# Three bias rows as one-row products on TensorE, and a new order of a code transpose and of the steps before a top-51 choice

## The chip, the cores and the metric

The kernel runs on one core of one Trainium2 chip. The metric is the device time of one execution in microseconds (us), the median of the runs shown. The engines are named as in the profile: PE is TensorE (PEld its weight loads), DVE is VectorE, ACT is ScalarE, POOL is GpSimd, SP is SyncE, whose queue issues most DMAs.

## The reference

Four layers of gated cross attention with a feed-forward part behind each, float32, on `x` of 8 batches by 256 rows by 128 columns, with 16 heads of 8 columns and a context of the same shape. Cut to the skeleton, and to the two parts of layer 3 that the change touches:

```python
for l in range(4):
    x = x + tanh(g_xattn[l]) * xattn_l(layernorm(x), ctx)
    x = x + tanh(g_ffn[l])   * ffn_l(layernorm(x))

# xattn_3: attention of the chosen rows only
q, k, v = proj(queries, Wq, bq), proj(keys, Wk, bk), proj(values, Wv, bv)
mean_scores = einsum('bhqd,bhkd->bhqk', q / norm(q), k / norm(k)).mean(-1)
_, top_idx = top_k(mean_scores, 51)                  # 256 // 5
ctx_sel = softmax(q[top_idx] @ k.T / sqrt(8)) @ v
context = zeros.at[top_idx].set(ctx_sel)
out = context @ Wo.T + bo

# ffn_3: x and the weight rounded to a 6-bit grid in blocks of 32
out = (grid(x) * scales) @ (grid(W) * scales).T + bias
```

ffn_2 is a mixture of 8 experts, two for each row, plus one shared block: `out + gelu(xf @ ws1 + bs1) @ ws2 + bs2`, where each expert's bias `b2` is weighted by the row's combine weights.

## The kernel before

The stream `xs` stays in SBUF as 16 tiles of 128 rows by 128 columns, two for each of 8 batches; `xnT` holds the turned norm, for 512 rows at a time per pair of batches (`pairs`, m = 0 to 3). All PSUM work goes through 8 banks (`one_bank`).

The order of instructions is written out by hand. A `Plan` holds a list of beats. Each beat has a `base` (functions in a fixed order) and an `extra` (functions that `put` places where room is left, or that `force` sets into a beat), and `run` calls base then extra, beat after beat. What a function issues goes onto its engines' queues in that order, so an instruction that waits holds everything behind it on the same engine.

By the profile's time the stages are: to about 400 us layers 0 and 1 with their feed-forward parts; to 556 layer 2's attention; 556 to 603 the way into the experts; 603 to 691 the 39 tiles of the experts; 691 to 743 the rest of the shared block, layer 3's norms and the choice of the rows; 743 to the end layer 3's attention and feed-forward part.

*556 to 603.* The router of layer 2 for the last batches (`route2`: logits, L676; best two, their places in the experts' tables by products with a mask, L807 and L809; labels copied by ACT, L834; rows sent out by indexed DMAs on POOL, L785), the keys of layer 3 (`keys`, L342 and L344, squares L1086, L1092) and the shared block for pair 0 (`fill[0]`). A shared block has eight units: four `shared_hidden` (product L1014, Gelu on ACT L1017) and four `shared_project` (products L1032, then L1035 that adds the bias weighted by the combine weights, joined to `xs` by DVE L1038). The first `shared_project` also turns the combine weights `cmb` (four products, L1024) and copies them to `cmbT` on ACT (L1028). The norm of batch 7 is in this stage as well: DVE's Newton steps, L308 on ACT, the turn `turn_norm` as product L326 and copy L327. The first expert tile begins with the product of L961.

*716 to 732.* Layer 3's norm goes pair by pair: statistics on DVE (L283, L284), `apply` on ACT (L308, four of 128x128 a pair), `turn_norm` (L326, L327). For the choice, `square_queries(m)` projects the queries (L1133) and squares them (ACT L1135); `lengths(ms)` sums the squares by head for two pairs (L1144) and takes the reciprocal on DVE (L1148); `cosines(ms)` multiplies `xnT` by the mean of the unit keys (L1155), takes the size on ACT (L1160) and ranks on DVE (L1161, L1162). `choose` starts with the first DVE MAX8 at L1176.

*743 to the end.* `PLACE3` is the order within a round of layer 3: a round has steps of batches i-4 to i+2. The steps that the text names: `vals` (the values of a batch, products L381, copy L387, bias L390 on POOL), `bias` (`add_row` of `ob[:, 3, :]`, POOL L331), `output` (`add_to_x`: the stream by the identity, L530, plus the context by the weight, L532, copied back by ACT L535), the norm (`stats`, `first`, `steps_` L265 to L268 on POOL for batches 0 to 5 and on DVE for 6 and 7, the mean times scale L298 and L299, `apply` L308 on ACT), `add_row` of `frow[:, 1, :]` (L331), the rounding to the grid (`scales` L1400 to L1405 on DVE, `units_` L1410, `step` L1415 to L1417, `scale_` L1420 and L1421, `near` L1424, `off` L1427, `lower_` L1431, `sized` L1434, those without an engine named on POOL for batches 0 to 5 and on DVE for 6 and 7), `turn_` (L1464, copy L1466), and `out_` (`add_to_x` again and the store to HBM). The one-hot matrices `one_hot_back` (DVE L1253, 128x2048) and `one_hot` (DVE L1258, 128x1632) and the attention's own steps (scores L1325, maxima L457, the denominators L1353 to L1361, the scatter back L1376, its copy `cT` L1381) stand between them.

Of the kernel before, what the change touches and what calls it, by code (L numbers as in the profile page):

```python
# [17 lines left out]
P = 128  # L18
NB = 8
S = 256  # L20
# [68 lines left out]
def tile_gated_cross_attention_stack(ctx: ExitStack, tc: tile.TileContext, ins: dict, out: bass.AP):  # L89
# [179 lines left out]

    norm = {}  # L270

    def layer_norm(bs, row=None, eng=None, out_eng=None, lag=2, wait=1):
# [12 lines left out]

        def first():
            v = tiny("v", [P, 4])[:, 0 : 2 * n]
            V.tensor_scalar(v, got["mv"][:, :, 1], LN_EPS, None, ALU.add)
            got["y"] = *guess(v, 2 * n, f"ln{n}"), v

        def steps_():
            y, t_, v = got["y"]
            newton(y, t_, v, eng)
            m = tiny("m", [P, 4])[:, 0 : 2 * n]
            if eng is V:
                V.scalar_tensor_tensor(m, got["mv"][:, :, 0], -1.0, y, ALU.mult, ALU.mult)  # L296
            else:
                eng.tensor_tensor(m, got["mv"][:, :, 0], y, ALU.mult)  # L298
                eng.tensor_scalar(m, m, -1.0, 0.0, ALU.mult, ALU.add)  # L299
            got["m"] = m  # L300

        def apply(k):
            t = norm[bs[k]] = moe.tile([P, 2, ROW], F32, tag="xn", name="xn", bufs=8)
            for i in range(2):
                c = slice(2 * k + i, 2 * k + i + 1)
                o, x, y, m = t[:, i, 0:D], xs[:, 2 * bs[k] + i, :], got["y"][0][:, c], got["m"][:, c]
                if out_eng is A:
                    A.activation(o, x, AF.Identity, bias=m, scale=y)  # L308
                else:
                    eng.tensor_scalar(o, x, y, m, ALU.mult, ALU.add)  # L310

        e = "V" if eng is V else "G"
        todo = [(1, dict(V=0.7), stats, k) for k in range(n)]
        todo += [(1, dict(V=0.5), first), (1, {e: 2.8 if eng is G else 1.9}, steps_)]
        todo += [
            ((wait if eng is G else 1) if k == 0 else 1, dict(A=0.7) if out_eng is A else {e: 0.9}, apply, k) for k in range(n)
        ]
        todo += [(lag if k == 0 else 0, dict(T=0.45, A=0.37), turn_norm, b) for k, b in enumerate(bs)]
        if row is not None:
            todo += [(0, dict(G=0.73), add_row, b, row) for b in bs]  # L320
        return todo
# [45 lines left out]
    def queries(l, m):  # L367
        t = project(l, m, 0, xnT)
        for g in range(NG):
# [5 lines left out]
                )  # L375
            qs[l, m, g] = o

    def vals(l, b):
        ps = one_bank()
        for c in range(2):  # L380
            nc.tensor.matmul(  # L381
                ps[:, c * P : (c + 1) * P], lhsT=ctxT[:, b * S + c * P : b * S + (c + 1) * P], rhs=wvo[:, l, 0, :],
                start=True, stop=True,
            )
        o = vaug[b % 2][:, :, :, 0:HD]
        ps = ps[:, 0:S].rearrange("p (c h d) -> p c h d", c=2, d=HD)
        A.copy(o, ps)  # L387
        if l == NL - 1:
            for c in range(2):
                G.tensor_tensor(o[:, c], o[:, c], bv3.rearrange("p (h d) -> p h d", d=HD), ALU.add)  # L390

    def mask(ps, w):

# [130 lines left out]
        xb = xs[:, 2 * b : 2 * b + 2, :].rearrange("p t d -> p (t d)")  # L524
        V.scalar_tensor_tensor(xb, px[:, 0:S], gate(l, False), xb, ALU.mult, ALU.add)

    def add_to_x(b, xT, w):

        px, xb = one_bank(), xs[:, 2 * b : 2 * b + 2, :].rearrange("p t d -> p (t d)")
        nc.tensor.matmul(px[:, 0:S], lhsT=ident, rhs=xb, start=True, stop=False)  # L530
        for c in range(2):
            nc.tensor.matmul(  # L532
                px[:, c * P : (c + 1) * P], lhsT=xT[:, c * P : (c + 1) * P], rhs=w, start=False, stop=c == 1
            )
        A.copy(xb, px[:, 0:S])  # L535

    def output3(b):
        add_to_x(b, cts.pop((NL - 1, b)), wvo[:, NL - 1, 1, :])

    def before_steps(n):  # L540

# [466 lines left out]
    def shared_hidden(blk, ch):  # L1008
# [7 lines left out]
        )  # L1016
        A.activation(shared[blk][:, ch, :], ps, AF.Gelu, bias=b1[:, NE, ch : ch + 1])  # L1017

    def shared_project(blk, i):
        t, hT = 4 * blk + i, shared[blk]  # L1020
        if i == 0:
            ps = one_bank()
            for k in range(4):
                nc.tensor.matmul(  # L1024
                    ps[0:NE, k * P : (k + 1) * P], lhsT=cmb[:, 4 * blk + k, :], rhs=ident, start=True, stop=True
                )
            cT = work.tile([P, 512], F32, tag="sy", name="cmbT", bufs=2)[0:NE, :]
            A.copy(cT, ps[0:NE, :])  # L1028
            shared[blk, "c"] = cT
# [5 lines left out]
        nc.tensor.matmul(  # L1035
            ps[:, 0:D], lhsT=shared[blk, "c"][:, i * P : (i + 1) * P], rhs=b2, start=False, stop=True
        )
        V.tensor_tensor(xs[:, t, :], xs[:, t, :], ps[:, 0:D], ALU.add)  # L1038
# [98 lines left out]
    def lengths(ms):  # L1137

        if ms[0] == 0:
            rank3["sc"], rank3["size"] = work2("sc"), work2("size")  # L1140
        o, ps = slice(32 * ms[0], 32 * ms[0] + 64), one_bank()
        for k in range(2):
            for m in ms:
                nc.tensor.matmul(  # L1144
                    ps[32 * m : 32 * m + 32, 0:S], lhsT=head_sum[:, k, :, :].rearrange("p k h -> p (k h)"),
                    rhs=squared[m][:, k * S : (k + 1) * S], start=k == 0, stop=k == 1,
                )
        V.reciprocal(rank3["sc"][o], ps[o, 0:S])  # L1148

    def cosines(ms):  # L1150

        o, ps = slice(32 * ms[0], 32 * ms[0] + 64), one_bank()
        for k in range(2):
            for m in ms:
                nc.tensor.matmul(  # L1155
                    ps[32 * m : 32 * m + 32, 0:S], lhsT=mean_w[:, m, k, :, :].rearrange("p k h -> p (k h)"),
                    rhs=xnT[:, m * 512 + k * S : m * 512 + (k + 1) * S], start=k == 0, stop=k == 1,
                )
        sc, size = rank3["sc"][o], rank3["size"][o]
# [298 lines left out]
    def ffn3(b, eng=None):  # L1458
# [8 lines left out]

        def out_():
            xb = xs[:, 2 * b : 2 * b + 2, :]
            add_to_x(b, got["rT"], w3T)  # L1470
# [191 lines left out]
    def last(t):  # L1662
        return slot, order2, 8, t

    for base in (
        (last(1),), (fill[0][0], last(3)), (fill[0][1], last(5)), (fill[0][2], last(7), fill[0][3]),
        ((keys, 3, 0), (keys, 3, 1)), ((keys, 3, 2),), (fill[0][4],), (fill[0][5],),
        ((keys, 3, 3), (square, 0), fill[0][6], (square, 1), fill[0][7], (squares, 0), fill[1][0]),
        ((square, 2), fill[1][1], (squares, 1), (square, 3), fill[1][2], (squares, 2), fill[1][3], (squares, 3)),
    ):  # L1670
        beat(*base)
# [30 lines left out]
    for i in range(TILES + 2):  # L1702
# [17 lines left out]
    order3 = [(3, b) for b in range(NB)]  # L1720
    h2, p2, h3, p3 = fill[2][0:4], fill[2][4:], fill[3][0:4], fill[3][4:]
    lns = [
        {p[2].__name__ + str(p[3] if p[2].__name__ in ("apply", "stats") else ""): p[2:] for p in layer_norm(pair, ob[:, 3, :], G if m in (0, 1, 2) else V, A)}
        for m, pair in enumerate(pairs)
    ]

# [13 lines left out]
    for base in (  # L1740
        [(take, b) for b in range(NB)] + h2 + joins(0, V), p2[0:2] + statistics(0), p2[2:4] + h3 + joins(1, V),
        statistics(1) + joins(2, V) + p3[0:2] + applied(0), turned_(0) + statistics(2) + p3[2:4] + applied(1) + [(square_queries, 0)],
        turned_(1) + joins(3, V) + [(square_queries, 1)], statistics(3), applied(2), turned_(2) + applied(3) + [(square_queries, 2)],
        [(lengths, (0, 1)), (cosines, (0, 1))], turned_(3) + [(square_queries, 3)],
        [(lengths, (2, 3)), (cosines, (2, 3))],
    ):
        beat(*base)
    def last_norm(*a):
# [19 lines left out]
    for i in range(-1, NB + 4):  # L1768
# [75 lines left out]
```

## Time and profile before

| | |
|---|---|
| median of the runs (lowest, highest) | 872.11 us (871.02, 877.95) |
| the profiled execution's own time | 872.14 us |
| its span | 870.4 us |
| mean granted clock of PE | 0.933 |
| instructions | 23085 |

The page of the profile gives one execution: each engine's busy time, the span cut into 40 slices, the chain of waits that ended last, and the costliest groups. In the slices below each digit is a busy share in tenths, PEclk the granted clock of PE in tenths.

```profile
PE   4999999999999999999999998859999995587775
PEld 2666667666766666666776676535998861465553
DVE  7978889898886578767656675746687576578886
ACT  2567777777776522222665563635455542354442
POOL 3425478777433205022522235574455540048771
PEclk7999999999999999999999996978999996698885
```

A slice is 21.8 us. PE has 8 or 9 tenths until slice 33, but for slices 25 to 27 (the way into the experts); from slice 34 on (the choice, layer 3's attention) it has 5 to 8 and DVE and POOL are as busy as it is. The groups of the instructions that the change moves or removes:

| line, engine | what | count | each, us |
|---|---|---|---|
| L390 POOL | bias on the values of layer 3 | 16 | 0.458 |
| L331 POOL | a row added to two tiles of `xs` (32 with `ob`, 16 with `frow`, over all layers) | 48 | 0.73 |
| L530 PE | the stream by the identity into the bank, 128x256 | 32 records | 0.483 |
| L1148 DVE | reciprocal 64x256 | 2 | 1.76 |
| L308 ACT | the norm applied to one tile | 64 | 0.487 |

A float32 product shows as two records in the trace, so 16 calls of L530 are 32 records.

### The profile page before, as it was taken

How to read it: one execution, taken by the hardware profiler on the slowest of the kernel's cores; microseconds unless marked ns; L12 is line 12 of the kernel's file. 1: busy time of each engine (PE TensorE's matmuls, PEld its weight loads, DVE VectorE, ACT ScalarE, POOL GpSimd, SP SyncE). 2: the span in 40 equal slices, each digit the busy share in tenths (PEclk: the TensorE clock that was granted, in tenths of full speed). 3: DMA queues.
4: the chain of work that ended last, by engine and by line, in shares of the span. 5: the costliest groups of instructions: out<-in, count | busy, mean ns of one | idle time of the engine just before them, and what ended most of it. 6: DMA issues, size and time to landing. Idle time of an engine off the chain costs nothing.

```text
span 870.4 us, 23085 instructions
## 1 busy us (share of the span) xinstructions
PE 776.4 (89%) x8682; PEld 555.2 (64%) x8682; DVE 640.5 (74%) x1972; ACT 444.3 (51%) x1111; POOL 387.9 (45%) x1022
## 2 busy tenths in 40 slices
PE   4999999999999999999999998859999995587775
PEld 2666667666766666666776676535998861465553
DVE  7978889898886578767656675746687576578886
ACT  2567777777776522222665563635455542354442
POOL 3425478777433205022522235574455540048771
PEclk7999999999999999999999996978999996698885
DMA  4314333222220000010100100324576330553430
GB/s 121 103 52 101 86 86 93 62 66 64 65 56 3 1 1 1 2 24 2 27 15 15 27 10 21 110 80 126 145 201 184 94 96 0 104 100 75 87 63 24
DMA packets 59758, 56.40 MB, mean 65 GB/s; under 512 B 7112, under 2 KB 48912, under 8 KB 59648
## 3 DMA queue, kind: packets, MB, share of 16 engines
q1 hardware_dynamic: 56944, 50.06, 22.9%
q0 software_dynamic: 2272, 4.72, 1.5%
q8 instruction: 69, 1.13, 0.6%
q14 instruction: 41, 0.34, 0.1%
q10 hardware_dynamic: 432, 0.15, 0.1%
HBM read 31.99 MB, written 15.16 MB: 54 GB/s over the span
## 4 chain that ended last, share of the span: by engine, by line
PE 66%; DVE 22%; ACT 4%; issue 4%; POOL 3%; DMA 2%; another core or an unknown queue 0%; SPq 0%; DVEq 0%; ACTq 0%
PE one L405 17%; PE one L485 8%; DVE nm L457 7%; PE one L745 4%; PE one L734 4%; PE one L735 4%; PE one L975 4%; PE one L1001 4%; PE one L342 3%; PE one L394 2%; PE one L1032 2%; PE one L521 1%; ACT e L460 1%; PE one L1014 1%; DVE back L1253 1%
## 5 line engine op out<-in xcount | busy, mean ns | idle before, releaser
L457 DVE TENSOR_REDUCE nm<-one 128x2 f32<-128x512 f32 (+1 forms) x416 | 240.6, 642 | 85.3 <-PE one L394 42.9
L460 ACT ACTIVATE e<-one 128x512 f32<-128x512 f32 (+1 forms) x384 | 185.9, 566 | 59.9 <-PE one L405 58.5
L405 PE MATMUL one<-q,k 32*128 32x256 f32 (+1 forms) x1536 | 191.1, 381 | 5.4 <-issue 1.6
L405 PE MATMUL one<-k,q 32*128 32x256 f32 (+1 forms) x1536 | 185.3, 387 | 3.2 <-DMA q<-proj 3.2
L405 PEld LDWEIGHTS one<-k,q 32*128 32x128 f32 x1536 | 133.3, 193 | 36.1 <-issue 15.2
L405 PEld LDWEIGHTS one<-q,k 32*128 32x128 f32 x1536 | 139.1, 189 | 16.2 <-issue 5.4
L485 PE MATMUL one<-e,vaug 128*32 128x256 f32 (+1 forms) x1536 | 87.3, 369 | 1.0 <-ACT e L460 0.9
L411 POOL TENSOR_SCALAR_AFFINE_SELECT e<-e 128x1024 f32<-128x1024 f32 x32 | 35.0, 1094 | 96.2 <-ACT e L460 80.4
L265 POOL TENSOR_TENSOR t_ln<-y_ln 128x2 f32<-128x2 f32 (+1 forms) x105 | 21.4, 204 | 104.0 <-DVE y_ln L255 98.5
L485 PEld LDWEIGHTS one<-e,vaug 128*32 128x32 f32 x1536 | 45.2, 111 | 33.8 <-DVE nm L457 5.1
L980 ACT ACTIVATE h<-one,tb 128x128 f32<-128x128 f32 x156 | 44.6, 370 | 41.2 <-PE one L975 36.9
L785 POOL DMA_INDIRECT done<-y,back_to x39 | 39.5, 1014 | 48.2 <-DVE xT L963 27.5
L737 ACT ACTIVATE act<-one 128x512 f32<-128x512 f32 x40 | 23.9, 597 | 61.0 <-PE one L734 56.0
L745 PEld LDWEIGHTS one<-ffn,act 128*128 128x128 f32 x320 | 41.2, 192 | 16.7 <-issue 14.1
L738 DVE TENSOR_TENSOR act<-act,one 128x512 f32<-128x512 f32 x40 | 27.4, 685 | 25.8 <-PE one L735 18.7
L491 ACT COPY u<-one 128x256 f32<-128x256 f32 x48 | 17.9, 374 | 48.9 <-PE one L485 48.4
L975 PE MATMUL one<-xT,k 128*128 128x128 f32 x312 | 41.5, 276 | 1.0 <-DVE xT L963 1.0
L308 ACT ACTIVATE xn<-xs,m,y_ln 128x128 f32<-128x128 f32 x64 | 27.7, 487 | 26.9 <-DVE m L296 17.2
L745 PE MATMUL one<-ffn,act 128*128 128x128 f32 x320 | 41.4, 275 | 0.0
L734 PE MATMUL one<-xnT,ffn 128*128 128x512 f32 x80 | 41.3, 598 | 0.0
L1001 PE MATMUL one<-w2all,h 128*128 x312 | 41.2, 276 | 0.0
L735 PE MATMUL one<-xnT,ffn 128*128 128x512 f32 x80 | 40.9, 592 | 0.0
(346 smaller groups left out, 1571.1 us busy)
## 6 DMA issues: line engine op xcount, KB each, us to landing
k<-in_w_dram SPq DMA_DIRECT2D x39, 256.0 KB
sent<-zero SPq DMA_DIRECT2D x34, 264.0 KB
back<-places SPq DMA_DIRECT2D x16, 512.0 KB
k<-proj SPq DMA_DIRECT2D x24, 128.0 KB
q<-proj SPq DMA_DIRECT2D x48, 64.0 KB
xt<-sent SPq DMA_DIRECT2D x39, 66.0 KB
w2all<-in_w_dram SPq DMA_DIRECT2D x4, 512.0 KB
yt<-done SPq DMA_DIRECT2D x8, 256.0 KB
```

Source lines behind the costliest of these rows:

```text
L405: nc.tensor.matmul(o, lhsT=a, rhs=r, start=alone_ or s == 0, stop=alone_)
L411: G.affine_select(d, d, pattern=[[0, 8], [1, P]], compare_op=ALU.is_ge, fill=0.0, base=0, channel_multiplier=-1)
L457: V.tensor_reduce(nm, ps.rearrange("p (s k) -> p s k", s=2), AX.X, ALU.max, negate=True)
L460: A.activation(e, ps[:, 0 : 2 * w].rearrange("p (s q) -> p s q", s=2), AF.Exp, scale=SCALE)
L485: nc.tensor.matmul(ps[strip(j), q0:S], lhsT=va[:, at : at + 32], rhs=e[:, c, j, s, 0 : S - q0], start=c == 0 and s == 0, stop=c == 1 and s ...
L734: nc.tensor.matmul(pa, lhsT=wa, rhs=toks, start=True, stop=True)
L735: nc.tensor.matmul(pb, lhsT=wb, rhs=toks, start=True, stop=True)
L745: nc.tensor.matmul(py[:, i * P : (i + 1) * P], lhsT=a[:, i * P : (i + 1) * P], rhs=w, start=n == 0, stop=n == len(ws) - 1,)
L785: i = G.indirect_dma_start(out=dst[:, :], out_offset=bass.IndirectOffsetOnAxis(ap=rows_, axis=0), in_=src, in_offset=None)
L975: nc.tensor.matmul(ps[:, ch * P : (ch + 1) * P], lhsT=wa[:, ch * P : (ch + 1) * P], rhs=turned[i][0], start=True, stop=True)
L980: A.activation(h[:, ch, :], ps[:, ch * P : (ch + 1) * P], AF.Gelu, bias=plan["tb"][:, i, ch : ch + 1])
L1001: nc.tensor.matmul(ps[:, 0:D], lhsT=h[:, ch, :], rhs=wb[:, ch, :], start=ch == 0, stop=ch == NCH - 1)
```

## The change

Three things are changed.

1. *Bias rows.* A new function `row_to` adds a row to all 128 partitions of a bank by a product: a row of ones (one partition by 128 columns) as the weights, the row itself, seen twice, as the moving part. It runs 24 times, all in layer 3: in `vals` ahead of the two products of L381 (with `bv3`; the products then accumulate on it), and in `add_to_x` between L530 and the products of L532, in `output3` with `ob[:, 3, :]` and in `out_` with `frow[:, 1, :]`. The POOL instructions that did the same are gone: L390 for the values, `add_row` for the other two in layer 3.
2. *Shared block's codes.* The turn of the combine weights (L1024, L1028) becomes `shared_codes(blk)`. For pair 0 it runs three beats earlier, after the third `shared_hidden` and before the last slot of layer 2's attention; other pairs keep their place. Two units of the shared block move as well: `fill[0][5]` and `fill[0][6]` each one beat earlier, and `fill[1][0]` ahead of `squares` of pair 0.
3. *Way to the choice.* `lengths` and `cosines` keep their products only; the reciprocal becomes `inverse(ms)` and the size and ranking `ranked(ms)`. The products for pairs 0 and 1 now come ahead of the norm's last apply and of the turns of pairs 2 and 3, and the two later steps behind those turns. For pair 3 the second batch's `apply` is on DVE (`vector_too=(1,)`) instead of ACT. SP's order of DMAs stays what it was.

```diff
+    def row_to(ps, row, start=False):
+
+        nc.tensor.matmul(
+            ps[:, 0:S].rearrange("p (c d) -> p c d", c=2), lhsT=ones[0:1, 0:P],
+            rhs=row[0:1].unsqueeze(1).to_broadcast([1, 2, D]), start=start, stop=False,
+        )
+
     def vals(l, b):
         ps = one_bank()
+        last = l == NL - 1
+        if last:
+            row_to(ps, bv3, True)
         for c in range(2):
             nc.tensor.matmul(
                 ps[:, c * P : (c + 1) * P], lhsT=ctxT[:, b * S + c * P : b * S + (c + 1) * P], rhs=wvo[:, l, 0, :],
-                start=True, stop=True,
+                start=not last, stop=not last or c == 1,
             )
...
         A.copy(o, ps)
-        if l == NL - 1:
-            for c in range(2):
-                G.tensor_tensor(o[:, c], o[:, c], bv3.rearrange("p (h d) -> p h d", d=HD), ALU.add)
...
-    def add_to_x(b, xT, w):
+    def add_to_x(b, xT, w, row):
...
         nc.tensor.matmul(px[:, 0:S], lhsT=ident, rhs=xb, start=True, stop=False)
+        row_to(px, row)
...
     def output3(b):
-        add_to_x(b, cts.pop((NL - 1, b)), wvo[:, NL - 1, 1, :])
+        add_to_x(b, cts.pop((NL - 1, b)), wvo[:, NL - 1, 1, :], ob[:, NL - 1, :])
...
+    def shared_codes(blk):
+        ps = one_bank()
+        for k in range(4):
+            nc.tensor.matmul(
+                ps[0:NE, k * P : (k + 1) * P], lhsT=cmb[:, 4 * blk + k, :], rhs=ident, start=True, stop=True
+            )
+        cT = work.tile([P, 512], F32, tag="sy", name="cmbT", bufs=2)[0:NE, :]
+        A.copy(cT, ps[0:NE, :])
+        shared[blk, "c"] = cT
+
     def shared_project(blk, i):
...
-        if i == 0:
...
+        if i == 0 and (blk, "c") not in shared:
+            shared_codes(blk)
...
-        V.reciprocal(rank3["sc"][o], ps[o, 0:S])
+
+    def inverse(ms):
+        o = slice(32 * ms[0], 32 * ms[0] + 64)
+        V.reciprocal(rank3["sc"][o], rank3.pop(("n2", ms))[o, 0:S])
...
-        (last(1),), (fill[0][0], last(3)), (fill[0][1], last(5)), (fill[0][2], last(7), fill[0][3]),
-        ((keys, 3, 0), (keys, 3, 1)), ((keys, 3, 2),), (fill[0][4],), (fill[0][5],),
-        ((keys, 3, 3), (square, 0), fill[0][6], (square, 1), fill[0][7], (squares, 0), fill[1][0]),
+        (last(1),), (fill[0][0], last(3)), (fill[0][1], last(5)), (fill[0][2], (shared_codes, 0), last(7), fill[0][3]),
+        ((keys, 3, 0), (keys, 3, 1)), ((keys, 3, 2),), (fill[0][4], fill[0][5]), (fill[0][6],),
+        ((keys, 3, 3), (square, 0), (square, 1), fill[0][7], fill[1][0], (squares, 0)),
...
-        turned_(1) + joins(3, V) + [(square_queries, 1)], statistics(3), applied(2), turned_(2) + applied(3) + [(square_queries, 2)],
-        [(lengths, (0, 1)), (cosines, (0, 1))], turned_(3) + [(square_queries, 3)],
-        [(lengths, (2, 3)), (cosines, (2, 3))],
+        turned_(1) + joins(3, V) + [(square_queries, 1)], statistics(3) + applied(2), [(lengths, (0, 1)), (cosines, (0, 1))],
+        applied(3) + turned_(2) + turned_(3) + [(inverse, (0, 1)), (ranked, (0, 1)), (square_queries, 2), (square_queries, 3)],
+        [(lengths, (2, 3)), (cosines, (2, 3)), (inverse, (2, 3)), (ranked, (2, 3))],
...
-        for p in last_norm((b,), frow[:, 1, :], eng, A) + ffn3(b, eng):
+        for p in last_norm((b,), None, eng, A) + ffn3(b, eng):
...
-        what["bias", b] = add_row, b, ob[:, NL - 1, :]
```

More of the change, by code (lines that the diff above doesn't have):

```diff
@@ L270, in tile_gated_cross_attention_stack, with layer_norm @@
     norm = {}
-    def layer_norm(bs, row=None, eng=None, out_eng=None, lag=2, wait=1):
+    def layer_norm(bs, row=None, eng=None, out_eng=None, lag=2, wait=1, vector_too=()):
         n = len(bs)
@@ L306, in apply @@
                 o, x, y, m = t[:, i, 0:D], xs[:, 2 * bs[k] + i, :], got["y"][0][:, c], got["m"][:, c]
-                if out_eng is A:
+                if out_eng is A and k not in vector_too:
                     A.activation(o, x, AF.Identity, bias=m, scale=y)
@@ L1017, in shared_hidden @@
         A.activation(shared[blk][:, ch, :], ps, AF.Gelu, bias=b1[:, NE, ch : ch + 1])
+    def shared_codes(blk):
[7 more added lines that the diff above has]
+        shared[blk, "c"] = cT
     def shared_project(blk, i):
         t, hT = 4 * blk + i, shared[blk]
-        if i == 0:
[L1022 to L1029, printed above, removed]
+        if i == 0 and (blk, "c") not in shared:
+            shared_codes(blk)
         ps = one_bank()
@@ L1140, in lengths @@
             rank3["sc"], rank3["size"] = work2("sc"), work2("size")
-        o, ps = slice(32 * ms[0], 32 * ms[0] + 64), one_bank()
+        ps = rank3["n2", ms] = one_bank()
         for k in range(2):
@@ L1147, in lengths @@
                 )
-        V.reciprocal(rank3["sc"][o], ps[o, 0:S])
+    def inverse(ms):
+        o = slice(32 * ms[0], 32 * ms[0] + 64)
+        V.reciprocal(rank3["sc"][o], rank3.pop(("n2", ms))[o, 0:S])
     def cosines(ms):
-        o, ps = slice(32 * ms[0], 32 * ms[0] + 64), one_bank()
+        ps = rank3["dot", ms] = one_bank()
         for k in range(2):
@@ L1158, in cosines, with ranked @@
                 )
+    def ranked(ms):
+        o, ps = slice(32 * ms[0], 32 * ms[0] + 64), rank3.pop(("dot", ms))
         sc, size = rank3["sc"][o], rank3["size"][o]
@@ L1469, in out_ @@
             xb = xs[:, 2 * b : 2 * b + 2, :]
-            add_to_x(b, got["rT"], w3T)
+            add_to_x(b, got["rT"], w3T, frow[:, 1, :])
             nc.sync.dma_start(out=out_tiles[:, 2 * b : 2 * b + 2, :], in_=xb)
@@ L1722, in tile_gated_cross_attention_stack @@
     lns = [
-        {p[2].__name__ + str(p[3] if p[2].__name__ in ("apply", "stats") else ""): p[2:] for p in layer_norm(pair, ob[:, 3, :], G if m in (0, 1, 2) else V, A)}
+        {p[2].__name__ + str(p[3] if p[2].__name__ in ("apply", "stats") else ""): p[2:] for p in layer_norm(pair, ob[:, 3, :], *((G, A) if m < 3 else (V, A)), vector_too=(1,) if m == 3 else ())}
         for m, pair in enumerate(pairs)
```

## The prediction

> **What bounds the kernel now.** I read the page first: the busy shares and the chain of waits. Columns of the first line are busy time, share of the span and instructions of each engine.
>
> ```profile
> PE 776.4 (89%) x8682; PEld 555.2 (64%) x8682; DVE 640.5 (74%) x1972; ACT 444.3 (51%) x1111; POOL 387.9 (45%) x1022
> ...
> PE 66%; DVE 22%; ACT 4%; issue 4%; POOL 3%; DMA 2%; another core or an unknown queue 0%; SPq 0%; DVEq 0%; ACTq 0%
> ```
>
> TensorE leads as an average, so work put on it looks bad and work put on POOL looks free. The change, though, touches only four stretches, and there the engines stand differently. A table by stretch (start:end, length, then busy time of PE, PE's weight loads, DVE, ACT and POOL, then granted clock, DMA share and GB/s):
>
> ```profile
> 556.00:603.00 47.00, 36.48 (x191) 21.25 (x183) 29.07 (x150) 20.20 (x57) 32.41 (x68) 0.79 0.39 121
> 716.00:732.30 16.30, 11.79 (x45) 4.33 (x44) 7.83 (x22) 7.41 (x17) 0.39 (x2) 0.79 0.00 0
> 777.70:842.00 64.30, 48.73 (x1009) 37.12 (x1008) 55.08 (x127) 29.83 (x88) 49.82 (x116) 0.87 0.45 90
> 842.00:870.40 28.40, 15.27 (x132) 11.18 (x132) 20.14 (x72) 7.93 (x21) 6.76 (x9) 0.68 0.08 24
> ```
>
> In the first two no engine is full: each is a chain that passes from engine to engine. In the rounds of layer 3's attention (third line) DVE (86%) and POOL (77%) are the full ones and PE has 15.6 us free; the last line is the tail. I take them in turn, by timelines (start, duration, engine, line, operation; in brackets the idle time before it and who ended it).
>
> **Shared block's codes ahead (556 to 603).**
>
> ```profile
> 582.08 0.56 ACT L1028 COPY cmbT<-one 8x512 f32<-8x512 f32 x1
> 582.69 0.50 PEld L1035 LDWEIGHTS one<-b,cmbT 8*128 8x128 f32 x2 [8.02 <-ACT cmbT L1028]
> 582.69 0.79 PE L1035 MATMUL one<-b,cmbT 8*128 8x128 f32 x2 [7.83 <-ACT cmbT L1028]
> ...
> 583.41 0.69 PE L326 MATMUL one<-ident,xn 128*128 128x128 f32 x2
> ```
>
> PE stands 7.83 us because the copy of the codes waits on ACT behind batch 7's norm, three projections (L344, the last ends at 582.18) and the router's labels. Behind it on PE stands L326, batch 7's turn, whose input was ready at about 578.8 (L308 ended then), and behind that the whole routing of batch 7. With the codes copied earlier PE passes L1035 at once and L326 runs near 578.9; ACT's copy L327 (584.14 before) stands now behind L344 and the labels, the last of which end at 582.18. So route 7 starts at about 582.1 instead of 584.14: 2.0 us. The start of the tiles (602.96) hangs on the last scatter of that route and the fetch behind it, and on PE's fills: the two fill products of 1.5 us that follow L676 now lie in the gap, so PE is free at about 599.4, the data there at about 600.0. I take −2.0. It costs 0.97 us of the transposes and of what is between them (571.03 to 572.00) ahead of batch 7's L521 on PE; DVE's L525 on it showed 1.96 us of idle put to no engine, which may hide it or not. If not, −1.0; if route 7's labels, too, move, −3. A copy ahead on ACT is 0.56 beside idle ACT. Half clock holds here from 576 to 592.5; with the gap filled that may lift, which is in the −3.
>
> **The way to the choice (716 to 732).**
>
> ```profile
> 719.41 2.07 PE L1133 MATMUL one<-xnT,wqp 128*128 128x512 f32 x2 [0.46 <-ACT xnT L327]
> 721.42 1.92 PE L1144 MATMUL one<-qsq,head_sum 128*32 128x256 f32 x8
> 723.12 1.92 PE L1155 MATMUL one<-xnT,mean_w 128*32 128x256 f32 x8
> 724.98 1.01 PE L326 MATMUL one<-ident,xn 128*128 128x128 f32 x4
> 726.45 1.12 PE L1133 MATMUL one<-xnT,wqp 128*128 128x512 f32 x2 [0.46 <-ACT xnT L327]
> ```
>
> One chain of products at half clock for most of it (the granted clock is 0.5 from 718.93 to 725.76). The second L326 (pair 3) stands behind L1144 and L1155 of pairs 0 and 1, although pair 3's norm ended on ACT at 720.9. After that come L1133 to 727.57, the square on ACT (727.62, 0.69), L1144, the reciprocal on DVE (729.45, 1.76), two DVE steps (731.24 to 732.18) and the choice at 732.22. The change puts pairs 0 and 1's lengths and cosines into the wait ahead of 717.47 (PE idle 1.16) and 719.41, on squares that were ready at 713.91 + 0.69 and 716.35 + 0.69 = 717.04. Worked through with the same durations: lengths 0 and 1 from 717.1, cosines to 720.1 (eight products took 1.70 at half clock, 721.42 to 723.12, and some 1.2 at full, where the last seven L1155 took 1.24), four turns to 721.3 (half of pair 3's norm on DVE, whose two steps stand where DVE is idle, instead of ACT's 1.65 at 719.26), L1133 twice to 723.4, squares to 724.2, L1144 to 725.1 at full clock, reciprocal 1.76, last two steps 0.95 with their gaps: choice at 728.1; at half clock throughout, 729.8. Against 732.22 that is −4.1 to −2.4. The first pair's reciprocal and DVE steps (1.76, 0.47, 0.42) go to where DVE waits. I take −3.7: the clock had come back by 725.76 before, with less dense work. Bounds −4.6 (if the denser work keeps full clock all through) and −2.2.
>
> **Three bias rows: POOL gives up.** 16 times L390 at 0.458 and 16 of L331 (ob and frow of layer 3) at about 0.73 leave POOL: 7.3 + 11.7 = 19.0 us. POOL is not on its own the end of a round: its Newton steps wait for DVE's seed (L255), and DVE then waits for ACT's norm. What the rows do is stand before POOL's quantising step L1410 and so let it fall on DVE's long L1253. Round at 778 (no frow row yet) and round at 803:
>
> ```profile
> 778.68 1.73 DVE L1253 TENSOR_SCALAR back<-back,lane 128x2048 f32<-128x2048 f32 x1
> ...
> 778.70 0.62 POOL L1410 TENSOR_TENSOR q_y<-xn,q_inv 128x256 f32<-128x256 f32 x1 [0.44 <-DVE q_inv L1404]
> ...
> 803.90 1.83 DVE L1253 TENSOR_SCALAR back<-back,lane 128x2048 f32<-128x2048 f32 x1
> 803.91 0.73 POOL L331 TENSOR_TENSOR xs<-xs,frow 128x256 f32<-128x256 f32 x1
> 804.60 1.61 POOL L1410 TENSOR_TENSOR q_y<-xn,q_inv 128x256 f32<-128x256 f32 x1
> ```
>
> With the row, L1410 takes 1.61 and the two block one another in turn. (The Trainium skill, "SBUF — State Buffer", section "Who interferes with whom", says that DVE and GpSimd share one port pair and that the one that issues first holds it for its whole instruction; these two rows agree.) From L1404's start to L1253's end is 2.05 us in the 778 round and 2.36 in the 803 one: −0.31. L1431 behind it takes 0.83 here and 0.42 where POOL is quiet (851.19): −0.41. L1416 at 0.72 against 0.29 stays, since L1434 moves with it. So about 0.65 a round, in five rounds (789, 802, 816, 828, 840): −3.3.
>
> **TensorE takes on.** 24 products of one row by 256 columns. Nothing in the trace has one contraction row. The nearest rows: a 128-row product of the same 256 columns, L530, whose first record to the next line takes 0.53 us at full clock and 0.85 at half (865.27 to 866.13); and L1035, eight rows, which takes 0.41 start to start where L1032's 128-row one takes 0.22, so that the small one is the dearer, perhaps by 0.2 for the change of rows. Below, nothing: a row of ones has no source that anybody waits for, except that A.copy of vals starts at the last product, so no gain but POOL's. I take 0.45 at full clock and 0.85 at half, and keep 0.7 and 1.1 as upper ends. (The Trainium skill, "TensorE: Matmul & The Clock Gate", section "Why this matters for your kernels", has it that a single product of few contraction rows takes the time of one of 128; by it the row is dear for what it computes, 0.53 like L530, and the sum below would be 0.1 worse for each row on the path.)
>
> In the rounds 3 rows a round are 1.3 to 2.6 us against some 3 us of PE's waits: the output row lies in the 0.83 us wait of L532 for cT (804.13), vals and ffn rows in waits of the score stage, 1.16 us at 802's L1353 to L1356 and 3 in 816's. In the two rounds at half clock I let 0.4 each come through: +0.8. At the ramp the first vals row stands before L381 (762.42) with PE the late engine: +0.45. In the tail batch 7's output row, between L530 (851.94) and L532 (852.96) at half clock, is bare, +0.85, and so is batch 7's ffn row between 865.27 and 866.13, +0.85; batch 6's hides, since L1464 waits for DVE until 864.79. L1403 at 859.46 took 0.34 beside POOL's row, else 0.17: −0.2. Tail +1.5.
>
> **Sum.** −2.0 −3.7 −3.3 +0.8 +0.45 +1.5 = −6.2 us. The profiled execution took 872.14 us (span 870.4 and 1.7 around it), and the median of the runs is 872.11, so nothing is to be shifted: 865.9, 0.7% less.
>
> **Rivals.**
> *TensorE becomes the bound of the rounds* (the slower side). If a row of one contraction row is never hidden, 24 × 0.43 = 10.3 us at full clock to 24 × 0.85 = 20.4 at half are added, with the rounds' gain gone; less 5.7 from the two chains that makes +4.6 to +14.7, 877 to 887. For it: PE is the first engine of the page, and clock 0.87 in the rounds. Against: 15.6 us of PE idle in 64.3, in which 15 rows need 6.5 to 12.8, and DVE busy 86%. It decides once a round's PE work, rows included, passes the 11.8 to 13.25 us of its loop. 0.12.
> *The chains' gain does not arrive, or the rounds' doesn't*: the choice at half clock throughout and the transition held by its labels, the last scatter or a wait that the trace put to nobody. Then −1 and −2.2, and rows with no net gain: 868.5 to 872.5. 0.17.
> *More than summed*: L298 on POOL took 1.68 instead of 0.20 in the rounds at 789 and 802 because DVE's L1258 began first. With POOL ahead it starts first: 1.3 more in each of two rounds or more; with the upper ends of both chains 859 to 862.5. 0.13.
> *The rows' removal moves nothing*: if the rounds' loop does not care for POOL's rows, the two chains (−5.7) and the price on PE (+2.75) leave −3, 869; it is counted with the second rival's 0.17.
>
> **How the numbers follow.** Forecast 862.5 to 868.5 with 0.58, likeliest 866. The range leaves out the upper part of the slower rival and a little of the better one: 860 to 875. About 1% is what a measurement here can tell from no change, 8.7 us: faster than 863.4 is the better rival (0.13) and the quick edge of the forecast (0.15); slower than 880.8 is half of the slower rival and some: 0.08. The rest, 0.64, is within it.
>
> **What would show it.** L1035's idle of 7.83 gone and the first tile's L961 near 600.5 instead of 602.96; choice's L1176 some 3.7 earlier by its distance from L1133 of pair 0; no POOL L331 or L390 in layer 3, L1410 at 0.62 and L1431 at 0.42; rounds of 11.2 to 12.6 us; tail longer by 1.5. Wrong would be: rounds longer with PE's idle gone (the rows), a row_to over 1 us, a choice that starts as late after pair 0's L1133 as before, or PE's wait at L1035 passed on to L326 or L676 in full.

## The result and the profile after

The changed kernel takes 865.3 us (median of 20 runs, 861.85 to 870.91) against 872.02 us (20 runs, 868.28 to 877.95): a ratio of 0.9925, 95% interval 0.9908 to 0.9941, or 6.7 us less. The profiled execution of it has a span of 866.2 us, 4.2 less than that of before; its own time, 868.21 us, lies 2.9 above its median; the second stretch below shows a wait of 4 us that may be the reason.

The page of the profile after, busy shares and chain of waits:

```profile
PE 798.9 (92%) x8730; PEld 564.8 (65%) x8730; DVE 633.8 (73%) x1974; ACT 442.7 (51%) x1109; POOL 367.0 (42%) x990
...
PE 70%; DVE 18%; ACT 3%; issue 3%; DMA 3%; POOL 2%; SPq 0%; DVEq 0%; ACTq 0%; POOLq 0%
```

PE has 48 records more (24 rows, two records each) and 22.5 us more of busy time, POOL 21 us less, and the kernel is faster: the page's averages say nothing about which of them mattered. A cut by stage does. Each length runs from one instruction's start to the next one's, in two profiles of each kernel (the second of each was taken later on, in the experiments below), beside the forecast; line numbers are those of before:

| stage | before | before, again | after | after, again | forecast |
|---|---|---|---|---|---|
| start to batch 7's L525 | 570.8 | 570.7 | 571.6 | 576.0 | 0 |
| to the first tile's L961 | 32.2 | 33.7 | 31.0 | 29.5 | -2.0 |
| to the last tile's | 83.7 | 84.7 | 83.7 | 84.5 | 0 |
| to the choice, L1176 | 45.6 | 45.4 | 40.4 | 40.4 | -3.7 |
| ramp, to batch 0's L1404 | 46.1 | 45.9 | 47.2 | 46.6 | +0.45 |
| six rounds, to batch 6's L1404 | 72.2 | 72.0 | 69.6 | 69.6 | -2.5 |
| tail, to the end | 19.9 | 19.9 | 22.8 | 22.8 | +1.5 |

From the choice on the stages repeat to a few tenths (the ramp least, 0.6). The first two do not: the first tile starts at 602.95 and 604.35 us in before and at 602.58 and 605.47 in after, so that the two kernels differ there by no more than two profiles of one of them.

**The way to the choice.** PE's timeline in the profile of after (L1144, L1155, L1169 are the L1133, L1144, L1155 of before):

```profile
714.79 1.12 PE L1144 MATMUL one<-xnT,wqp 128*128 128x512 f32 x2 [0.88 <-ACT xnT L327]
715.85 0.62 PE L1155 MATMUL one<-qsq,head_sum 128*32 128x256 f32 x2
716.70 0.83 PE L1155 MATMUL one<-qsq,head_sum 128*32 128x256 f32 x5 [0.23 <-ACT qsq L1146]
717.16 0.38 PE L1169 MATMUL one<-xnT,mean_w 128*32 128x256 f32 x1
717.37 0.38 PE L1155 MATMUL one<-qsq,head_sum 128*32 128x256 f32 x1
717.38 1.24 PE L1169 MATMUL one<-xnT,mean_w 128*32 128x256 f32 x7
718.54 1.49 PE L326 MATMUL one<-ident,xn 128*128 128x128 f32 x8
720.01 1.98 PE L1144 MATMUL one<-xnT,wqp 128*128 128x512 f32 x4
```

The eight products of pairs 0 and 1 (sixteen records), which took 721.42 to 725.04 before, lie now between 715.85 and 718.62 and at full clock (granted 1.00), where PE waited for the norm; the four turns of pairs 2 and 3 follow in one piece. The choice starts at 726.64.

**The codes.** The 7.83 us wait before L1035 is gone (L1046 runs at 575.72 behind L1043 without a wait), but another stands two instructions on. All engines, after:

```profile
577.63 0.44 PE L326 MATMUL one<-ident,xn 128*128 128x128 f32 x2
...
582.58 0.29 DVE L1049 TENSOR_TENSOR xs<-xs,one 128x128 f32<-128x128 f32 x1 [4.73 <-remote]
582.65 0.37 ACT L327 COPY xnT<-one 128x256 f32<-128x256 f32 x1 [4.03 <-remote]
...
583.07 1.02 PE L684 MATMUL one<-gw,xnT 128*128 128x8 f32 x4 [5.00 <-issue]
```

Batch 7's turn ends at 578.07, and the copy of it that ACT has next starts at 582.65. DVE's L1049, which waits for a product that ended at 577.70, starts at 582.58. For 4.0 us neither PE nor DVE nor ACT runs anything; only POOL works, on its indexed sends and three short steps. Such a stretch, in which the three engines stand at once, is called a standstill below.

**Rounds.** DVE and POOL in the 785 round (L1270, L1427 are L1253, L1410):

```profile
785.89 1.72 DVE L1270 TENSOR_SCALAR back<-back,lane 128x2048 f32<-128x2048 f32 x1
...
785.92 0.61 POOL L1427 TENSOR_TENSOR q_y<-xn,q_inv 128x256 f32<-128x256 f32 x1 [1.26 <-DVE q_inv L1421]
...
787.54 0.41 DVE L1448 SCALAR_TENSOR_TENSOR q_r<-q_t,q_r 128x256 f32<-128x256 f32 x1
```

In this round as forecast: 0.61 for POOL's step instead of 1.61, and 0.41 for L1448 (L1431 before) instead of 0.83. The next round is like it. The three behind them are not; the one at 810:

```profile
810.91 1.28 DVE L1270 TENSOR_SCALAR back<-back,lane 128x2048 f32<-128x2048 f32 x1
...
810.96 1.70 POOL L1427 TENSOR_TENSOR q_y<-xn,q_inv 128x256 f32<-128x256 f32 x1 [1.29 <-DVE q_inv L1421]
...
812.11 0.83 DVE L1448 SCALAR_TENSOR_TENSOR q_r<-q_t,q_r 128x256 f32<-128x256 f32 x1
```

Here POOL's step is held as long as before (1.70) and L1448 takes 0.83 as before; what is shorter is DVE's L1270, 1.28 instead of 1.83. The gain is the same: from L1404's start to L1431's end 3.11 us in before's 803 round, 2.38 in the 785 round here and 2.36 in the 810 round.

**Tail.** PE in the last batch, before:

```profile
865.27 1.06 PE L530 MATMUL one<-xs,ident 128*128 128x256 f32 x2
866.13 1.06 PE L532 MATMUL one<-w3T,rT 128*128 128x128 f32 x4
```

PE in the last two batches, after (L537, L540, L1481 are L530, L532, L1464; L380 is the row):

```profile
856.04 1.06 PE L537 MATMUL one<-xs,ident 128*128 128x256 f32 x2
857.03 1.22 PE L380 MATMUL one<-frow,ones 1*128 1x256 f32 x2
858.18 1.22 PE L540 MATMUL one<-w3T,rT 128*128 128x128 f32 x4
859.20 0.63 PE L1481 MATMUL one<-ident,q_r 128*128 128x128 f32 x2
859.62 1.06 PE L537 MATMUL one<-xs,ident 128*128 128x256 f32 x2
860.61 1.22 PE L380 MATMUL one<-frow,ones 1*128 1x256 f32 x2
```

L537 to L540 is 2.14 us; L530 to L532 was 0.86 before. A row costs 1.28 at half clock, not 0.85. The second L1481, batch 7's, comes at 859.20 although DVE's input for it was done at 858.74, so batch 6's row ahead of it was not hidden either.

### The profile page after: what moved, and what is told of

The parts are those of the page before. It is cut to its first block, busy times and chain, and to the rows that moved or that the text cites. A ratio compares the mean times of both kernels' runs of the same rounds, so it can differ in the third digit from the quotient of the medians.

```text
span 866.2 us, 23122 instructions
## 1 busy us (share of the span) xinstructions
PE 798.9 (92%) x8730; PEld 564.8 (65%) x8730; DVE 633.8 (73%) x1974; ACT 442.7 (51%) x1109; POOL 367.0 (42%) x990
## 4 chain that ended last, share of the span: by engine, by line
PE 70%; DVE 18%; ACT 3%; issue 3%; DMA 3%; POOL 2%; SPq 0%; DVEq 0%; ACTq 0%; POOLq 0%
PE one L412 18%; PE one L492 9%; DVE nm L464 6%; PE one L753 4%; PE one L742 4%; PE one L743 4%; PE one L983 4%; PE one L1009 4%; PE one L342 3%; PE one L401 2%; PE one L1043 2%; PE one L528 2%; ACT e L467 1%; PE one L1022 1%; PE one L380 1%
## 5 line engine op out<-in xcount | busy, mean ns | idle before, releaser
L464 DVE TENSOR_REDUCE nm<-one 128x2 f32<-128x512 f32 (+1 forms) x416 | 240.4, 640 | 92.5 <-PE one L401 47.2
L753 PEld LDWEIGHTS one<-ffn,act 128*128 128x128 f32 x320 | 41.2, 192 | 16.7 <-issue 14.1
L983 PEld LDWEIGHTS one<-xT,k 128*128 128x128 f32 x312 | 38.4, 193 | 1.3 <-DVE xT L971 1.3
```

The costliest lines, as they stand in the source:

```text
L464: V.tensor_reduce(nm, ps.rearrange("p (s k) -> p s k", s=2), AX.X, ALU.max, negate=True)
L753: nc.tensor.matmul(py[:, i * P : (i + 1) * P], lhsT=a[:, i * P : (i + 1) * P], rhs=w, start=n == 0, stop=n == len(ws) - 1,)
L983: nc.tensor.matmul(ps[:, ch * P : (ch + 1) * P], lhsT=wa[:, ch * P : (ch + 1) * P], rhs=turned[i][0], start=True, stop=True)
```

## The experiments

They ran in three groups, each on one chip, another one for each group, with the kernel before beside it. Before took 875.0 us in the first group, 866.9 in the second and 872.45 in the third, so whole times are compared by their ratio to the before of the same group.

**The three parts, each alone, and the whole again (first group).** Each kernel is the one before with that part of the diff only: the new base list, `inverse`, `ranked` and `vector_too` (e1); `shared_codes` and its place (e2); `row_to` and its three uses (e3).

> The kernel before with the new way to the choice alone. Theory (the profile of after: the choice starts 5.2 us earlier counted from the first tile): -5.0 us, ratio 0.994, the two L1148 reciprocals to the first MAX8 as in after, nothing changed ahead of 690 us and behind the choice. Rival (forecast's size): -3.7, 0.996. Rival (the gain hangs on the other two parts, for instance on the clock): less than -2, 0.998 or more.

Measured: 870.42 us, ratio 0.9943 (0.9914 to 0.9972), -4.6 us; choice 40.37 us behind the last tile, as in after. The theory holds by this stage (the interval of the time includes the rival's 0.996 as well), and the part needs neither of the others.

> The kernel before with the shared block's codes and fills moved alone. Theory: -2 to -3 us, ratio 0.997; PE's wait of 7.83 us ahead of L1035 is gone. Rival (the wait is passed on to batch 7's turn, as the 4 us wait of L327 in the profile of after suggests): -0.4 us, ratio 0.9995, with the 4 us wait in this profile too. If that wait is an accident of one execution it is absent here.

Measured: 873.77 us, 0.9991 (0.9961 to 1.0021). Time alone can't tell -2 from 0. The long wait is gone here too, and the standstill is there again, elsewhere: two pieces of 1.41 and 3.00 us between 573.74 and 578.73. It is no accident of one execution, but no fixed place either.

> The kernel before with the three bias rows on TensorE alone. Theory (intervals of after's profile: ramp +1.05, rounds -2.6, tail +2.9): +1.4 us, ratio 1.0015, tail about 1.3 us longer for each bare row at half clock. Rival (forecast): -0.55, 0.9994. Rival (TensorE bounds the rounds): +4 or more, 1.005.

Measured: 874.46 us, 0.9988 (0.9961 to 1.0015). By stage: six rounds 68.2 instead of 72.2, tail 22.2 instead of 19.9, ramp 46.2. So -4.0 and +2.3; no sign of a TensorE that bounds the rounds, and the sum of the theory is off by 3, because in the profile of after one round is 1.5 longer than here (below), the tail 0.6 and the ramp 1.0.

> The changed kernel once more, for a second profile and times on the same chip. All three parts: -6.7 us, ratio 0.9925. Theory: the 4 us in which DVE and ACT stand before 582.6 is an accident of one execution and is absent or elsewhere here, and the first tile starts 2 us or more ahead of that of before. Rival: it comes with the change and is at the same place again.

Measured: 868.33 us, 0.9916 (0.9885 to 0.9948). Stages as in the table. The product of the three single ratios is 0.9922: within the noise the parts add. The standstill is elsewhere, split in three (1.6 us at 529.6, 1.6 at 574.4, 1.4 at 596.6). The first tile, expected 2 us ahead of before's, starts at 605.5, behind it.

**What a row costs, and what it holds (second group).** In e5 the weights are a full tile `shares`, filled with 1/128 once:

```diff
-            ps[:, 0:S].rearrange("p (c d) -> p c d", c=2), lhsT=ones[0:1, 0:P],
-            rhs=row[0:1].unsqueeze(1).to_broadcast([1, 2, D]), start=start, stop=False,
+            ps[:, 0:S].rearrange("p (c d) -> p c d", c=2), lhsT=shares,
+            rhs=row.unsqueeze(1).to_broadcast([P, 2, D]), start=start, stop=False,
```

> The changed kernel with each bias row as a product of 128 contraction rows (weights all 1/128, the row present on every partition) instead of one. Theory (PE runs empty around a product of other height; in the profile of after a row adds 0.62 us at full clock and 1.29 at half, against 0.53 and 0.85 for the 128-row L530): the tail (from batch 6's L1421 to the end, 22.8 us in both profiles of the changed kernel) comes to 21.5, three bare rows by 0.44 each; in all -1.5 to -2.5 us against the changed kernel. Rival (few rows take the time of 128, the rest is loads and waits that stay): tail 22.6 or more, no difference in time. Rival (loading 128 rows of weights is dearer): tail over 23.

Measured: 856.56 us, 0.9897 (0.9862 to 0.9931); tail 19.26 (21.5 expected), shorter than before's 19.9. The row at full clock, in the changed kernel's round at 798:

```profile
798.33 0.70 PE L537 MATMUL one<-xs,ident 128*128 128x256 f32 x2
798.96 0.69 PE L380 MATMUL one<-ob,ones 1*128 1x256 f32 x2
799.58 0.71 PE L540 MATMUL one<-wvo,cT 128*128 128x128 f32 x4
```

PE's last batch in e5, at full clock too (line numbers one higher):

```profile
850.70 0.60 PE L538 MATMUL one<-xs,ident 128*128 128x256 f32 x2
851.13 0.59 PE L381 MATMUL one<-frow,shares 128*128 128x256 f32 x2
851.57 0.61 PE L541 MATMUL one<-w3T,rT 128*128 128x128 f32 x4
```

The row of 128 adds 0.44 here and 0.85 at half clock (848.45 to 849.30). The row of one added 0.72 at full clock (798.33 to 799.58 is 1.25, where L530 to L532 took 0.53 without it) and 1.28 to 1.30 at half. The page of the Trainium skill that the prediction names ("TensorE: Matmul & The Clock Gate", "Why this matters for your kernels") gives a single product of 32 contraction rows the time of one of 128. The measurements differ from that for a row of one between products of 128 rows: it is the dearer by half or more. The gain in the tail, 3.0 us against e8 (22.24, same group), is more than the 1.3 forecast, and the clock was higher too; how much of the rest is the clock's is not separated. Windows of the last two batches, this kernel first, then e8, whose rows and tail are those of the changed kernel (columns as in the prediction's table):

```profile
836.16:845.47 9.31, 6.58 (x38) 5.11 (x30) 7.18 (x30) 2.52 (x7) 0.72 (x1) 0.82 0.05 15
845.47:855.40 9.93, 4.83 (x20) 4.04 (x20) 4.49 (x14) 1.49 (x4) 0.00 (x0) 0.83 0.14 40
```

```profile
835.15:845.08 9.93, 7.69 (x42) 4.17 (x34) 7.19 (x31) 2.52 (x7) 0.72 (x1) 0.84 0.05 14
845.08:857.35 12.27, 7.39 (x20) 4.53 (x20) 4.49 (x14) 1.49 (x4) 0.00 (x0) 0.50 0.11 32
```

The granted clock in the last window is 0.83 with rows of 128 and 0.50 with rows of one.

In e6 six rows went back to POOL (TensorE keeps the values' for `b > 1`, the output's for `0 < b < 7`, the feed-forward part's for `b < 6`):

> The changed kernel with only the rows at the two edges given back to POOL: values of batches 0 and 1, output of 0 and 7, feed-forward of 6 and 7. Theory (the rows are bare at the edges and hidden in the rounds): tail back from 22.8 to 20.0 or 20.4, ramp (first MAX8 to batch 0's L1421) back from 46.6 to 47.2 to about 46.1, rounds as in after; -3 us against the changed kernel. Rival (POOL's rows hold DVE in the tail as they did in before): tail 21 or more.

Measured: 855.17 us, 0.9900 (0.9864 to 0.9936); tail 19.63, ramp 45.5 (e8: 45.9). The rows were bare in the tail, as the theory says; the ramp's 0.5 is hardly more than two profiles of one kernel differ by.

In e7 the mean times scale becomes one DVE step in `apply`, ahead of the one-hot step:

```diff
+            if late_mean:
+                V.scalar_tensor_tensor(got["m"], got["mv"][:, :, 0], -1.0, got["y"][0], ALU.mult, ALU.mult)
```

> The changed kernel with layer 3's mean times scale (L298 and L299 on POOL) as one DVE step ahead of L1275, for batches 0 to 5. Theory (L298 is held 1.5 us by DVE's one-hot step L1275 in three rounds, and DVE waits 1.3 us for the norm behind it): these three rounds go from 12.5 to 11.7, -2.4 us in all. Rival (TensorE is by now the end of a round): rounds stay at 12.4 to 12.5, and what DVE waits for is an ACT copy that waits for PE.

Measured: 856.35 us, 0.9887 (0.9857 to 0.9917); rounds 11.13, 11.88, 11.93, 11.19, 11.19 against e8's 11.74, 12.50, 12.56, 10.98, 11.02. The direction holds, with 0.6 instead of 0.8 in each of three rounds and 0.2 lost in two. In the changed kernel POOL's L298 was held in three rounds, as in before (the prediction named two), and here DVE's step is. First the changed kernel, then e7:

```profile
782.01 1.68 POOL L298 TENSOR_TENSOR m<-mv,y_ln 128x2 f32<-128x2 f32 x1
```

```profile
798.42 0.67 DVE L307 SCALAR_TENSOR_TENSOR m<-mv,y_ln 128x2 f32<-128x2 f32 x1
799.01 1.85 DVE L1279 TENSOR_TENSOR to<-chosen,u 128x1632 f32<-128x1632 f32 x1
```

L298 began 0.24 us behind DVE's L1275 (781.77). DVE's L307 began 0.08 behind POOL's 0.73 us subtraction of another batch (798.34) and now waits that out. Which of the two engines starts first decides who stands, as "SBUF — State Buffer" ("Who interferes with whom") of the Trainium skill has it.

> The changed kernel with all of pair 3's norm on ACT. Theory (DVE stands idle there and ACT does not): choice 0.6 to 0.9 us later than 40.37 us after the last tile's start. Rival (the reciprocal of pairs 0 and 1 on DVE was held up by as much): no difference, 40.2 to 40.5.

Measured: one run, 859.1 us; choice 41.12 us behind the last tile against 40.36. The theory holds: 0.76 us of the choice's gain comes from the half norm on DVE.

**The codes undone, and the best of both (third group).** e9 is the changed kernel without `shared_codes` and with the old order around it; e10 joins e5 and e7; e11 joins e5, e6 and e7.

> The changed kernel with the shared block's codes and fills where they were before. Theory (the codes' move is worth the forecast's 2 us where the stretch has no standstill of all engines, and its worth is drowned where it has): the transition (batch 7's L525 to the first tile) is 2 us longer than in the other kernels of this call that have the move (26.2 us in the four profiles of the last call), time 2 us over the changed kernel. Rival (moved wait: nothing gained): within 0.4 us of 26.2.

Measured: 868.37 us, 0.9944 (0.9915 to 0.9972), against 0.9925 and 0.9916 for the whole, measured on other chips: 1.7 to 2.4 us, with intervals that overlap. The transition (the table's second row) takes 32.2 us, against 30.9 and 31.5 in e10 and e11; but these two have standstills of 3.4 and 3.7 us in it, and e9 none longer than 0.6. So the second group's 26.2 was not the measure for this one, and neither side of the expectation is met.

> The changed kernel with both edits: bias rows as products of 128 rows, and the mean times scale on DVE. Theory (both add): rounds (five intervals) 56 to 57 us, tail 19.3, and 3 + 1.5 = 4.5 us less than the changed kernel; ratio to before about 0.986. Rival (TensorE bounds the rounds once they are shorter): rounds no shorter than e7_mean_dve's 66.7 for the first six, tail 19.3.

Measured: 859.76 us, 0.9854 (0.9820 to 0.9888), close to the 0.986 expected if both add; tail 18.1. The first five rounds take 57.4, above the 56 to 57 expected and no shorter than e7's 57.3, which is the rival's sign; but e5's 58.8 against e8's 58.8 shows that cheaper rows alone do not shorten the rounds, so this need not be TensorE. The six take 67.6: the sixth is 10.2 instead of e7's 9.4, at a granted clock of 0.71 instead of 0.99.

> As e10, with the rows at the two edges on POOL as in e6. Theory (a 128-row product at an edge costs less than POOL's hold on DVE): tail 19.6 against 19.3, ramp the same or 0.4 shorter, so no better than e10. Rival (bare rows cost whatever their height): 0.5 to 1 us better than e10.

Measured: 860.69 us, 0.9845 (0.9807 to 0.9883); tail 19.4, ramp 44.3 against 45.0. By time no different from e10: the ramp wins 0.7, the tail loses 1.2.

> The kernel before, for a second profile beside the others of this call. Theory: choice 44.0 to 45.6 us after the last tile's start (40.36 in the changed kernel), rounds 11.77, 13.25, 13.25, 11.84, 11.84, 10.2 and tail 19.9 as in the first profile, to within 0.2; transition as in e9 to within 1 us. Rival: the rounds or the tail of the first profile were accidents of that execution.

Measured: rounds 11.74, 13.23, 13.22, 11.81, 11.79, 10.22, tail 19.88, choice 45.37; transition 33.7, 1.5 off e9's and so outside the 1 us expected. The stages from the choice on belong to the kernel, not to one execution.

## Why the prediction was right

*Sum.* 6.2 us were forecast, 6.7 measured (interval 5.1 to 8.0, from the ratio). It holds as a sum, and that is partly luck: the choice gained 1.4 more than forecast and the tail lost 1.4 more. In the profiles the stages from the choice on add to about -3.8 (-5.1 +0.9 -2.5 +2.9); where the other 3 us of the medians' gain lie, no profile shows.

*Choice, -3.7.* The mechanism was right and the size too small: -5.0 to -5.2 between the profiles with the full kernels, -4.6 by e1's time. The stage's gain lies beyond the bound of -4.6 that was to cover full clock all through. Clock and order can be told apart in part by e2 and e3, which have before's order: there the stage took 44.2 and 44.0 us at a granted clock of 0.90 (from 16.7 us ahead of the choice to the choice), in before 45.6 and 45.4 at 0.80, in after 40.4 at 1.00 in both profiles. So before's order is 1.2 to 1.5 us shorter at 0.90 than at 0.80, and the other 3.7 are the new order and one more tenth of clock together. All ten kernels with the new order show 1.00 in this stretch; that the denser products keep the clock there fits, but no run changed the density alone. The half norm on DVE is 0.76 of the gain (e8).

*Rounds, -3.3 + 0.8.* -2.4 to -2.6 in the profiles of the changed kernel, near the -2.5 forecast, in part by luck. The reason given (L1410 no longer behind the row, L1431 no longer beside POOL) is what two of the five relieved rounds show. In the other three POOL is held as before and it is DVE's L1253 that runs free, for the same gain. Who goes first can't be read from starts this close: in the 785 round DVE's record begins 0.03 us ahead of POOL's and DVE is the one held, in the 810 round 0.05 ahead and POOL is. The prediction's two rows start 0.01 apart, so they agree with its rule by their lengths and not by their order. A relieved round gains 0.71 to 0.87 instead of 0.65, which makes -4.0 in e3, e8 and e9. What takes 1.5 of it back in the changed kernel is one round: 12.46 us in both its profiles, 10.98 to 11.00 in e3, e5, e6, e8 and e9. Windows of that round, after and e9:

```profile
810.59:823.05 12.46, 12.22 (x190) 8.28 (x190) 9.18 (x25) 6.03 (x19) 7.13 (x19) 0.73 0.42 81
```

```profile
813.00:823.98 10.98, 9.45 (x199) 6.67 (x202) 9.00 (x24) 6.12 (x19) 7.14 (x19) 1.00 0.47 96
```

TensorE was granted 0.73 in it (0.50 from 811.57 to 818.40) and was busy for 12.22 of 12.46 us; the five other kernels have 1.00. There the rival of TensorE as bound came true, once, with the half clock that the forecast's +0.8 stood for. ACT's timeline of the same round in after:

```profile
820.12 0.37 ACT L397 COPY vaug<-one 128x256 f32<-128x256 f32 x1 [0.90 <-PE one L391]
...
821.48 0.87 ACT L308 ACTIVATE xn<-xs,m,y_ln 128x128 f32<-128x128 f32 x2
```

The norm L308 had its input from POOL at 819.96 (L299, 819.77 + 0.19) and stood 1.5 us on ACT behind copies that waited for PE. Why the clock fell in this round in both profiles of the changed kernel and in none of the five others, the record does not show.

*Tail, +1.5, and rows.* This is the term that was mis-sized: +2.9. A one-row product was put at 0.45 and 0.85 with upper ends of 0.7 and 1.1; it costs 0.72 and 1.28. The prediction had seen the eight-row L1035 take 0.41 where the 128-row product takes 0.22, and took the row nearest in columns (L530), not the one nearest in contraction rows. At 1.28 batch 7's two rows give 2.6, and batch 6's, said to hide, adds 0.46. The other kernels with one-row products in the tail show +2.3 to +2.8 (e3, e8, e9). In e5 the same rows, 128 high, cost 0.44 and 0.85 at the same clocks, and the tail is 19.3, with a share of the clock in it.

*Ramp, +0.45.* 47.2 and 46.6 in the two profiles of after against 46.1 and 45.9 in before, but 46.2, 45.9 and 46.2 in e3, e8 and e9 with the same rows: not settled beyond "between nothing and +1.3".

*Codes, -2.0.* PE's wait before L1035 went, as forecast, in every kernel with the move; without it the wait is there (7.8 to 9.6 us). But the sign named for the gain, a first tile near 600.5, did not come: 602.6 and 605.5. In the first profile of after PE waits 5.0 us ahead of L684 (L676 before) instead, close to what the prediction called a sign of being wrong. In e8, where no long standstill came, L684 followed L326 by 1.84 us, which is quicker than the forecast's 3.6 (578.9 to ACT's copy at 582.1 and its 0.4); in after it was 5.4. Over the ten profiles that are not of the second group the first tile starts at 602.6, 605.5, 606.3, 599.3 and 604.8 with the move and 603.0, 604.4, 609.6, 610.5 and 605.2 without: means 603.7 and 606.5, which fits a gain of 2. But the five without the move have one and the same program up to there and are 7.5 us apart, so it is not shown. Nor is it excluded that the move itself invites a standstill: all five with it have one of 1.6 us or more behind 570 us, and of the five without it e3 alone (the others 1.0 or less).

*Open.* What the engines stand for is not known. It lies where POOL sends rows by indexed DMA, the waits end on DVE and ACT up to 5 us after the product they wait for, it comes with and without the change (0.9 us at most at once in the second profile of before, 8.0 us in e3, in three pieces, 1.2 or less in the second group's four), and it moves between executions. No kernel here took a suspected cause of it away, and the codes' move was not profiled against its absence on the second group's chip.

## What to carry to other kernels

Price an added product by the nearest row in contraction height as well as in columns: a bias as a one-row product between 128-row ones cost 0.72 us at full clock where the same sum as a 128-row product cost 0.44. Work moved off a helper engine is worth what it held on others (here DVE's long step and POOL's own next one), and is paid for at the edges of a pipeline, where the receiving engine is bare and its clock low. Judge a part by the length of its own stage: choice, rounds and tail repeated here to 0.2 us in two profiles of a kernel while whole executions differed by 9. And read the granted clock of a stage before putting its length down to the order of its work.

## What had not been expected of the hardware

The granted clock in the last 10 us was 0.83 in the two kernels whose tail has 128-row rows (e5, e10) and 0.50 to 0.56 in all twelve others, at nearly the same busy time as the kernels without rows there (4.83 us in e5, 4.73 in before). And the part ahead of the choice differs by group: the first tile starts at 592.2 to 594.6 us in the second group's four profiles, which all have the codes' move, and at 599.3 to 606.3 in the five others that have it. Batch 4's L525 of layer 2 comes at 516 to 521 us in all; batch 5's, 21.5 to 21.8 us later in the second group's four, 23.5 to 25.7 in the ten others. The difference arises where POOL's indexed sends run. Whether the chip makes it is open, since each chip served one group. Part of it is lost again: the stage of the tiles takes 86.8 to 87.6 us in the second group and 83.7 to 84.7 in the others.
